# Encoder states loaded with channels first instead of transposed by TensorE

## The chip, the cores and the metric

The kernel runs on one core of a Trainium2 chip. The metric is device time in microseconds, the median of several executions. The core has five engines, each with its own queue of instructions: TensorE (PE, with its weight loads shown as PEld), VectorE (DVE), ScalarE (ACT), GpSimd (POOL) and SyncE (SP), which here only issues DMA transfers. Transfers run on 16 DMA engines.

## The reference, cut to what matters

The kernel is one decoder layer on x of shape (32, 128, 128), with a second input ctx_768 of shape (32, 128, 96), the encoder states. Everything is float32.

```
x = x + attn(layernorm(x))             # linear attention over 16 heads, gated
x = x + xattn(layernorm(x), ctx_768)   # the part that the change touches
x = x + ffn(layernorm(x))              # shared expert + one of 8 routed experts

def xattn(h, e, Wq, Wk, Wv, Wo, bo):   # h (32,128,128), e (32,128,96)
    q, k, v = h @ Wq, e @ Wk, e @ Wv   # 1024 wide: 16 heads of 64
    p = softmax(q @ k.T / 8) per head
    return (p @ v) @ Wo + bo
```

Keys and values are both products of the encoder states e with weights. On TensorE both operands of a product have the summed dimension on the partitions. For keys and values that is the channel of e (96), so the kernel needs e with channels first: `eT`, 96 partitions, and along the free dimension the positions of the group's four batch entries.

## The kernel before, in words

The 32 batch entries go in 8 groups of 4 (`NG`, `GT`); a group has 4 x 128 = 512 tokens (`GW`). Each group goes through self-attention (`attention`), the layer norm and query transposition for cross-attention (`prologue`), cross-attention proper, and the router (`router`); the expert part follows when all groups are routed.

Cross-attention is a loop over 64 steps, one for each group, half of the heads and batch entry, two steps per iteration (`for a in range(0, n, 2)`); a group so takes four iterations. An iteration computes scores, the maximum, exponentials, the division on POOL, the transposition of the probabilities, the mix with the values and the projection. Into fixed places of it (`place("S1")`, `place("P1")`, ...) go pieces of self-attention and prologue of the group two ahead and of the router of a group behind. `keys` for step a + 6 and `values` for the step itself are the products that read `eT`: so the first read of a group's `eT` is three iterations ahead of its own steps, and the last is `values` of its last step.

The order on PE, DVE, ACT and POOL is written out by hand: the wrapper `InTurn` (line 40, under which the profile shows all these instructions) ties each instruction of an engine behind the one before. SP's order is left to the framework's planner. In the trace SP issues what has nothing to wait for well ahead of its place in the code.

The encoder states before: `load_e(g)` (L229) loads a group of e as it lies, tokens on partitions, into `eg`, two buffers. Group 0's four blocks are transposed on TensorE by `encoder`; those of the other groups in step P2 of `attention(g)`, into the second bank of the PSUM pair that also holds the output projection (`oep`). In step E3 ACT copies them to `eT` (two buffers), and the load of the group two ahead is issued. On SP there are also the loads of x, the weights, and `clear_sorted`: 66 transfers of 264 KB that fill the DRAM table `xsort` (L324), into which POOL later scatters token rows (`indirect_dma_start` in `router`), each behind the clears ahead of it in the code.

Of the kernel before, what the change touches and what calls it, by code (L numbers as in the profile page):

```python
# [10 lines left out]
F32 = mybir.dt.float32  # L11
# [39 lines left out]
def kernel(  # L51
# [31 lines left out]
    nc = tc.nc  # L83
    B, S, D = x.shape
    DE = enc.shape[2]
# [7 lines left out]
    GT = 4  # L93
    NG = B // GT
    GW = GT * S
# [106 lines left out]
    pe = second_part.enter_context(tc.tile_pool(name="pe", bufs=2))  # L202
# [18 lines left out]
    bq_c = column(a_bq, "bq_c", nc.scalar)  # L221


    eg_of = {}

    def load_e(g):
        if g < NG:
            t = pe.tile([P, GT, DE], F32, tag="eg", name=f"eg{g}")
            nc.sync.dma_start(  # L229
                out=t, in_=enc[g * GT : (g + 1) * GT].rearrange("b s d -> s b d")  # L230
            )
            eg_of[g] = t
# [84 lines left out]
    def clear_sorted(g):  # L317

        n = GT * S
        first = [e * CAP + g * n for e in range(NE)]  # L320
        if g == NG - 1:
            first += range(NE * CAP, NROW, n)
        for r in first:
            ins = nc.sync.dma_start(  # L324
                out=xsort[r : r + n].rearrange("(p k) d -> p k d", p=P), in_=zeros
            )
            for put in sorted_by:
                tc.declare_no_dep(ins.ins, put.ins, reason="those rows lie in front")
            cleared_by.append(ins)
# [53 lines left out]
    def transposed(src, n, rows, name, ps=None, first=0):  # L383

        ps = bank(name) if ps is None else ps
        for t in range(first, first + n):
            pe_.transpose(ps[0:rows, t * P : (t + 1) * P], src[:, t, :], ident)
        return ps
# [15 lines left out]
    def attention(g, fixed=None):  # L404
# [73 lines left out]
        for a in range(2):  # L478
            nd2 = nd4[:, a, 0 : 2 * W].rearrange("p (b w) -> p b w", b=2)
            for b in range(2):  # L480
                t = 2 * a + b
# [47 lines left out]
        yield "E3"  # L529
        turned = None  # L530
        if g not in eT_of:
            eT_of[g] = pe.tile([DE, GW], F32, tag="eT", name=f"eT{g}")
            turned = act_.copy(eT_of[g], ep[0:DE, :])
            load_e(g + 2)
        ob = pa.tile([P, GT, D], F32, tag="ob", name=f"ob{g}")
        made = dve.tensor_tensor(
            ob, op4, bo_a.unsqueeze(1).to_broadcast([P, GT, D]), ALU.add
# [9 lines left out]


    steps = [(g, s, b) for g in range(NG) for s in range(2) for b in range(GT)]
    eT_of, xnT_of, qk_of, asked = {}, {}, {}, set()  # L550

    def encoder(g, evict):

        eT = pe.tile([DE, GW], F32, tag="eT", name=f"eT{g}")
        eT_of[g] = eT
        evict(eT, transposed(eg_of[g], GT, DE, f"eTp{g}")[0:DE, :])
        load_e(g + 2)

    def prologue(g, fixed=None):

# [31 lines left out]
    def queries(g, s, j):  # L592

        cols = slice((4 * s + j) * P, (4 * s + j + 1) * P)
        asked.add((g, s, j))
        qp = bank(f"xqp{g}_{s}_{j}")
        pe_.matmul(qp, lhsT=wq_x[:, cols], rhs=xnT_of[g], start=True, stop=True)
        act_.activation(qk_of[g, s, j][:, 0, :], qp, AF.Copy, scale=QSCALE)
# [17 lines left out]
    def scores(k):  # L616

        g, s, b = steps[k]
        rows = slice(b * S, (b + 1) * S)

        sc = pair(k % 2, f"sc{k}")
        for j in range(4):
            for p in range(2):
                half = slice(p * DH, (p + 1) * DH)
                pe_.matmul(
                    sc[:, p, j * P : (j + 1) * P],
                    lhsT=qk_of[g, s, j][half, 0, rows],
                    rhs=qk_of[g, s, j][half, 1, rows],
                    start=True,
                    stop=True,  # L630
                )
        sc_of[k] = sc

    def largest(k):
        sc = sc_of[k]
        nmax = small.tile([P, 8], F32, tag="nmax", name=f"nmax{k}")
        dve.tensor_reduce(
            nmax,
            sc.rearrange("p a (j k) -> p (a j) k", j=4),
            AX.X,  # L640
            ALU.max,
            negate=True,
        )
        pr_of[k] = pb.tile([P, 2, 4, P], F32, tag="pr", name=f"pr{k}")
        sums_of[k] = small.tile([P, 8], F32, tag="sums", name=f"sums{k}")
        sc_of[k] = sc, nmax
# [28 lines left out]
    def mix(k):  # L675

        av = bank(f"avp{k}")
        v, prT = v_of.pop(k), prT_of.pop(k)
        for j in range(4):
            for p in range(2):  # L680
                h = 2 * j + p
                pe_.matmul(
                    av[p * DH : (p + 1) * DH, j * P : (j + 1) * P],
                    lhsT=v[:, h * DH : (h + 1) * DH],
                    rhs=prT[:, p, j * P : (j + 1) * P],
                    start=True,
                    stop=True,
                )
        oT_of[k] = pb.tile([P, 4, S], F32, tag="oT", name=f"oT{k}")
        dve.tensor_copy(oT_of[k].rearrange("p j s -> p (j s)"), av)  # L690
# [436 lines left out]
    def place(*which):  # L1127
        for at in which:
            for one in list(beside):
                if one[0] == at:  # L1130
                    one[0] = next(one[1], None)
                    if one[0] is None:
                        beside.remove(one)
                        if one[2] is not None:
                            begin(one[2]())
# [69 lines left out]
    for a in range(0, n, 2):  # L1205
        both = (a, a + 1)
        scores(a)
        scores(a + 1)
        largest(a)
        place("S1")  # L1210
        if a:
            mix(a - 2)
            mix(a - 1)
        place("S3")
        largest(a + 1)
        exponentials(a)
        for k in both:
            if k + GT < n and steps[k + GT] not in asked:
                queries(*steps[k + GT])
        place("M1")  # L1220
        divide(a)
        if a:
            project(a - 2)
            project(a - 1)

            if a % 8 == 2 and 2 < a < n - 8 or a == n - 8:
                begin(router(steps[a - 1 if a == n - 8 else a - 3][0]))
        for k in both:
            if k not in v_of:
                values(k)  # L1230
        side["now"] = 0
        place("P1")
        if a >= n - 4:
            within["pair"] = 0
            products()
        exponentials(a + 1)
        divide(a + 1)
        place("E2")
        if a == n - 2:
            next(begun[0][1])  # L1240
        if a == 0:
            for k in (GT + 2, GT + 3):
                queries(*steps[k])
        for k in both:
            if k + GT + 2 < n and steps[k + GT + 2] not in qk_of:
                keys(*steps[k + GT + 2], act_.copy)
            if k == a:
                turn(a)
        if a == 0:
            values(2)  # L1250
        if a == n - 2:
            early = router(NG - 1, slice(0, GT // 2))
            next(early)
            next(early)
        place("S2", "M2")
        side["now"] = 1
        place("P2")
        if a >= n - 6:
            within["pair"] = 1
            products()  # L1260
        place("E3")
        if a == n - 2:
            next(begun[1][1])
            finish()
        while begun and a < n - 2:
            finish()
        turn(a + 1)
        if a == 0:
            place("S1")
        if a % 8 == 2:  # L1270
            clear_sorted(a // 8)
            g = a // 8 + 2
            if g < NG:
                begin(attention(g), lambda g=g: prologue(g))
        if a == 12:
            load_ffn()
        if a == n - 8:

            first_part.close()
            pools["g"] = ctx.enter_context(tc.tile_pool(name="pg", bufs=2, side="right"))  # L1280
            pools["c"] = ctx.enter_context(tc.tile_pool(name="pc", bufs=4, side="right"))
            pd = ctx.enter_context(tc.tile_pool(name="pd", bufs=1, side="right"))
            pools["down"] = pd.tile([P, NE, NC, D], F32, tag="wdr", name="wdr")
            for c in range(NC):
                nc.sync.dma_start(
                    out=pools["down"][:, :, c],
                    in_=rt_down[:, c * P : (c + 1) * P, :].rearrange("e p d -> p e d"),
                )
            whole_experts(pd, "up", rt_up)

            pieces += [
                (g, down(g) if c is None else hidden(g, c))
                for g, c in (
                    (0, 0), (0, 1), (1, 0), (1, 1), (2, 0), (2, 1), (0, None),
                    (3, 0), (3, 1), (1, None), (2, None), (3, None),
                )
            ]
# [198 lines left out]
```

## Time and profile before

| what | us |
|---|---|
| median of 3 runs | 613.0 (612.84 to 614.5) |
| the profiled execution | 612.94 |
| its span | 611.2 |
| PE busy | 594.8 |
| DVE busy | 443.0 |
| ACT busy | 390.9 |
| POOL busy | 247.9 |
| granted TensorE clock | 1.0 of full speed |

How to read it: busy is the time in which an engine has an instruction in work; weight loads (PEld) overlap products (PE). The span is that of the profiled instructions. In views of waits, `A <- B` reads "A stood idle until B was done". An `L40` in front of an engine's name is the wrapper's line, so instructions are told apart by the tiles that they write and read, `out<-in`. For DMA the page gives queues (q1 is SP's, q10 ACT's, q0 POOL's) with packets, megabytes, and the share of 16 engines' time that the packets took. In the first 75 us of the span the DMA engines are nearly full with the loads of x and weights and the clears; from then to about 410 us they are nearly idle, with 1 to 25 GB/s.

### The profile page before, as it was taken

How to read it: one execution, taken by the hardware profiler on the slowest of the kernel's cores; microseconds unless marked ns; L12 is line 12 of the kernel's file. 1: busy time of each engine (PE TensorE's matmuls, PEld its weight loads, DVE VectorE, ACT ScalarE, POOL GpSimd, SP SyncE). 2: the span in 40 equal slices, each digit the busy share in tenths (PEclk: the TensorE clock that was granted, in tenths of full speed). 3: DMA queues.
4: the chain of work that ended last, by engine and by line, in shares of the span. 5: the costliest groups of instructions: out<-in, count | busy, mean ns of one | idle time of the engine just before them, and what ended most of it. 6: DMA issues, size and time to landing. Idle time of an engine off the chain costs nothing. (4 is left out here: it accounts for less than half of the span.)

```text
span 611.2 us, 13300 instructions
## 1 busy us (share of the span) xinstructions
PE 594.8 (97%) x4681; PEld 449.6 (74%) x4681; DVE 443.0 (72%) x1226; ACT 390.9 (64%) x1414; POOL 247.9 (41%) x248
## 2 busy tenths in 40 slices
PE   8999999999999999999999999999999999899997
PEld 7546777776777777776777777767777777699965
DVE  5757667868877787778786878697776687866645
ACT  3376776777677767776777677766766676256521
POOL 3133423433544344424452445244434344346651
PEclk9999999999999999999999999999999999999999
DMA  6999900000000000000000000005000002054137
GB/s 161 304 354 352 354 25 2 14 2 1 10 23 1 1 11 23 1 2 10 23 2 1 10 10 1 1 11 146 2 2 10 10 10 79 28 119 118 49 101 210
DMA packets 42659, 39.64 MB, mean 65 GB/s; under 512 B 8592, under 2 KB 32656, under 8 KB 42592
## 3 DMA queue, kind: packets, MB, share of 16 engines
q1 hardware_dynamic: 39168, 33.80, 18.3%
q0 software_dynamic: 2144, 4.46, 2.2%
q8 instruction: 38, 0.62, 0.4%
q10 hardware_dynamic: 1280, 0.53, 0.4%
q14 instruction: 29, 0.24, 0.1%
HBM read 14.37 MB, written 24.40 MB: 63 GB/s over the span
## 5 line engine op out<-in xcount | busy, mean ns | idle before, releaser
L40 ACT ACTIVATE pr<-sc,nmax 128x128 f32<-128x128 f32 x512 | 180.5, 387 | 46.6 <-DVE nmax L40 43.7
L40 POOL TENSOR_TENSOR pr<-pr,rs 128x1024 f32<-128x1024 f32 x64 | 121.2, 1897 | 140.0 <-DVE x L40 87.8
L40 ACT ACTIVATION_READ_ACCUMULATOR pr<-sc,nmax 128x1 f32 x512 | 115.7, 226 | 0.0
L40 DVE TENSOR_REDUCE nmax<-sc 128x8 f32<-128x1024 f32 x64 | 77.9, 1218 | 12.7 <-PE sc L40 12.6
L40 PEld LDWEIGHTS xyp<-wo_x,oT 128*128 128x128 f32 x512 | 61.9, 192 | 14.1 <-issue 13.4
L40 PE MATMUL sc<-qk 64*128 64x128 f32 x1024 | 66.0, 279 | 0.7 <-DVE act L40 0.7
L40 PE MATMUL xkp<-eT,wk_x 96*128 96x512 f32 x128 | 65.1, 593 | 0.0
L40 PEld LDWEIGHTS sc<-qk 64*128 64x128 f32 x1024 | 59.9, 187 | 6.7 <-issue 5.0
L40 PE MATMUL xqp<-xnT_b,wq_x 128*128 128x512 f32 x128 | 63.1, 617 | 0.7 <-ACT xnT_b L40 0.7
L40 PE MATMUL avp<-prT,v 128*64 128x128 f32 x1024 | 63.2, 276 | 0.0
L40 PE MATMUL xyp<-wo_x,oT 128*128 128x128 f32 x512 | 62.7, 276 | 0.1
L40 PE MATMUL vp<-wv_x,eT 96*128 96x512 f32 x128 | 60.5, 593 | 0.8 <-ACT qk L40 0.8
L40 PEld LDWEIGHTS avp<-prT,v 128*64 128x64 f32 x1024 | 55.2, 137 | 4.1 <-issue 0.2
L40 ACT COPY prT<-prTb 128x512 f32<-128x512 f32 x64 | 37.6, 588 | 31.3 <-PE prTb L40 31.3
L40 DVE COPY prT<-prTa 128x512 f32<-128x512 f32 x64 | 43.8, 686 | 17.1 <-PE prTa L40 16.7
L40 ACT COPY qk<-xkp 128x512 f32<-128x512 f32 x64 | 37.7, 589 | 28.9 <-PE xkp L40 28.4
L40 DVE COPY v<-vp 128x512 f32<-128x512 f32 x64 | 43.4, 689 | 16.1 <-PE vp L40 16.1
L40 PEld LDWEIGHTS prTa<-ident,pr 128*128 128x128 f32 x256 | 30.6, 141 | 30.1 <-issue 16.7
L40 DVE COPY oT<-avp 128x512 f32<-128x512 f32 x64 | 42.2, 685 | 4.8 <-PE avp L40 4.6
L40 POOL DMA_INDIRECT ytok<-yt,rows x35 | 33.6, 961 | 25.8 <-DVE rows L40 23.7
L40 POOL DMA_INDIRECT xsort<-xs,row x32 | 32.4, 1012 | 20.9 <-issue 8.8
L40 PE MATMUL prTa<-ident,pr 128*128 128x128 f32 x256 | 39.1, 275 | 1.4 <-POOL pr L40 1.3
(170 smaller groups left out, 1010.0 us busy)
## 6 DMA issues: line engine op xcount, KB each, us to landing
xsort<-zeros SPq DMA_DIRECT2D x66, 264.0 KB, 4.0
xt<-xsort SPq DMA_DIRECT2D x39, 66.0 KB, 2.2
yg<-ytok SPq DMA_DIRECT2D x8, 256.0 KB, 4.8
x<-in_x_dram SPq DMA_DIRECT2D x7, 256.0 KB, 5.3
out_dram<-x SPq DMA_DIRECT2D x7, 256.0 KB, 4.9
eg<-in_ctx_dram SPq DMA_DIRECT2D x8, 192.0 KB, 3.3
wdr<-in_L_ffn_rt_down_dram SPq DMA_DIRECT2D x2, 512.0 KB
up<-in_L_ffn_rt_up_dram SPq DMA_DIRECT2D x1, 1024.0 KB, 9.2
```

Of the source, the lines that this page charges most:

```text
L40: made = getattr(self.engine, name)(*operands, **more)
```

## The change

Groups 2 to 7 no longer load `eg`. For them `load_e` issues four transfers, one for each batch entry, that write `eT` itself: 96 partitions of 128 words each, where neighbouring words of a partition lie 384 bytes apart in DRAM. `eT` has three buffers instead of two. `load_e` is called once per group in the loop, at the end of its second iteration (a % 8 == 2), just ahead of the clears, instead of behind a transposition. In `attention`, the transposes and the ACT copy drop out wherever `eT_of` has the group, which is the case for groups 2 to 7; group 0 and group 1 are loaded and transposed as before.

```
     def load_e(g):
-        if g < NG:
+        if 2 <= g < NG:
+            t = pe.tile([DE, GT, S], F32, tag="eT", name=f"eT{g}", bufs=3)
+            for b in range(GT):
+                nc.sync.dma_start(
+                    out=t[:, b, :], in_=enc[g * GT + b].rearrange("s d -> d s")
+                )
+            eT_of[g] = t.rearrange("p b s -> p (b s)")
+        elif g < 2:
             t = pe.tile([P, GT, DE], F32, tag="eg", name=f"eg{g}")
...
         if g not in eT_of:
-            eT_of[g] = pe.tile([DE, GW], F32, tag="eT", name=f"eT{g}")
+            eT = pe.tile([DE, GT, S], F32, tag="eT", name=f"eT{g}", bufs=3)
+            eT_of[g] = eT.rearrange("p b s -> p (b s)")
             turned = act_.copy(eT_of[g], ep[0:DE, :])
-            load_e(g + 2)
...
     def encoder(g, evict):
-        eT = pe.tile([DE, GW], F32, tag="eT", name=f"eT{g}")
-        eT_of[g] = eT
+        eT = pe.tile([DE, GT, S], F32, tag="eT", name=f"eT{g}", bufs=3)
+        eT_of[g] = eT = eT.rearrange("p b s -> p (b s)")
         evict(eT, transposed(eg_of[g], GT, DE, f"eTp{g}")[0:DE, :])
-        load_e(g + 2)
...
         if a % 8 == 2:
+            load_e(a // 8 + 2)
             clear_sorted(a // 8)
```

More of the change, by code (lines that the diff above doesn't have):

```diff
@@ L221 @@
     bq_c = column(a_bq, "bq_c", nc.scalar)
-    eg_of = {}
+    eg_of, eT_of = {}, {}
     def load_e(g):
-        if g < NG:
+        if 2 <= g < NG:
[6 more added lines that the diff above has]
+        elif g < 2:
             t = pe.tile([P, GT, DE], F32, tag="eg", name=f"eg{g}")
@@ L549 @@
     steps = [(g, s, b) for g in range(NG) for s in range(2) for b in range(GT)]
-    eT_of, xnT_of, qk_of, asked = {}, {}, {}, set()
+    xnT_of, qk_of, asked = {}, {}, set()
     def encoder(g, evict):
-        eT = pe.tile([DE, GW], F32, tag="eT", name=f"eT{g}")
-        eT_of[g] = eT
+        eT = pe.tile([DE, GT, S], F32, tag="eT", name=f"eT{g}", bufs=3)
+        eT_of[g] = eT = eT.rearrange("p b s -> p (b s)")
         evict(eT, transposed(eg_of[g], GT, DE, f"eTp{g}")[0:DE, :])
-        load_e(g + 2)
     def prologue(g, fixed=None):
```

## The prediction

> **What bounds the kernel now.** I read the page's busy shares, then TensorE's (PE's) timeline around one transposition, the encoder tile, SP's timeline, and the DMA answers for two short stretches. From the page:
>
> ```profile
> PE 594.8 (97%) x4681; PEld 449.6 (74%) x4681; DVE 443.0 (72%) x1226; ACT 390.9 (64%) x1414; POOL 247.9 (41%) x248
> ```
>
> PE is busy nearly always, the others are not. Its timeline (start, length, what; no bracket at the end means no idle time before it), from 85 us on:
>
> ```profile
> 85.63 1.88 PE L40 MATMUL vp<-wv_x,eT 96*128 96x512 f32 x4
> ...
> 106.00 1.05 PE L40 MATMUL oep<-wo_a,gT 128*128 128x128 f32 x8
> 106.89 0.60 PE L40 MATMUL oep<-ident,eg 128*96 128x128 f32 x4
> 107.33 0.60 PE L40 MATMUL prTa<-ident,pr 128*128 128x128 f32 x4
> ...
> 117.94 1.02 PE L40 MATMUL xkp<-eT,wk_x 96*128 96x512 f32 x2
> ...
> 179.88 1.02 PE L40 MATMUL xkp<-eT,wk_x 96*128 96x512 f32 x2
> ...
> 427.63 1.02 PE L40 MATMUL xkp<-eT,wk_x 96*128 96x512 f32 x2
> ```
>
> Three things are to be seen. The four transposes of a group take PE from 106.89 to 107.33, 0.44 us, since they are pipelined. A group lasts 61.94 us (117.94 to 179.88). And 117.94, 179.88 and so on to 427.63 are the first key products of groups 2 to 7: the moments at which their eT must be there. The line at 85.63 holds the last products that read eT of group 0; they end near 87.5.
>
> The encoder tile, and SP's timeline:
>
> ```profile
> L40 PE MATMUL oep<-ident,eg x28: 272/273/273, 47.7 to 416.9; 128*96 128x128 f32 x28
> L229 SPq DMA_DIRECT2D eg<-in_ctx_dram x8: 368/390/711, 1.3 to 293.3; - x8
> ...
> DMA to landing us min/median/max: 2.6/3.3/8.6
> ```
> ```profile
> 22.75 0.37 SPq L229 DMA_DIRECT2D eg<-in_ctx_dram  x1
> 23.21 11.97 SPq L324 DMA_DIRECT2D xsort<-zeros  x16
> ...
> 54.76 20.59 SPq L324 DMA_DIRECT2D xsort<-zeros  x27
> 107.52 186.19 SPq L229 DMA_DIRECT2D eg<-in_ctx_dram  x4
> 418.81 0.99 SPq L1285 DMA_DIRECT2D wdr<-in_L_ffn_rt_down_dram  x2
> ```
>
> An encoder load lands in 3.3 us now and nobody feels it. SP issues everything that waits for nothing at once: the 66 clears of xsort are issued between 23 and 75 us, 52 us of moving, though the code has them spread over the groups. From 107 to 418 us SP has only four loads to issue.
>
> The DMA answer for 107.5 to 111.5 us, in which one encoder load moves alone, and for 9.6 to 9.8 us, where the one-column biases arrive, 4 bytes a packet:
>
> ```profile
> q1 hardware_dynamic: 528, 0.20, 20.8%
> ```
> ```profile
> DMA packets 54, 0.00 MB, mean 1 GB/s; under 512 B 54, under 2 KB 54, under 8 KB 54
> q1 hardware_dynamic: 54, 0.00, 12.6%
> ```
>
> The share is of 16 engines' time. A 384-byte row takes an engine 0.208 x 4 us x 16 / 528 = 25 ns. A 4-byte word takes it 0.126 x 0.2 us x 16 / 54 = 7.5 ns. But the words come only 54 in 0.2 us, 3.7 ns apart over all engines: one in 59 ns per engine, with the engine idle between.
>
> **The change part by part.**
>
> Removed on PE: 4 transposes in each of 6 groups (28 in the oep row are groups 1 to 7; group 1 keeps its own, as does group 0 outside the row). 6 x 0.44 = 2.6 us. From 62 to 120 us PE is busy 58.00 of 58.00 us, so what goes from its row goes from the time. Bounds: 0 if another engine steps in, 6 x 0.60 = 3.6 us if the four cost their whole span. I take 2.6, the distance between starts.
>
> Removed on ACT: six copies of eT at 0.584 us, 3.5 us. ACT is at 64% and PE does not wait for these copies; nothing. Off DVE: the sum ob waited for the transposes of the same PSUM pair (11.2 us over seven); it starts about 0.44 us sooner, as PE's next work does; nothing.
>
> Added and moved on SP: 24 loads for 6, 0.39 us each to issue, 9 us on a queue idle for 300 us; nothing, unless issuing so many words holds SP longer, which is then hidden behind the transfer itself. What stands behind them on SP are clears, the shared expert's weights, and from 418 us on the expert weights. No load waits for a TensorE transposition now, but from group 3 on each waits for the last reader of the buffer three groups back: 87.5 us for group 3, needed at 179.9, so 92 us of room, at one load per 61.9 us.
>
> The unknown is the transfer. Each load has 96 x 128 = 12,288 words; a group has 49,152, and 3,072 per engine. Call a group's time L. By the words' own 7.5 ns, L = 23 us. By the 25 ns of a strided row, L = 77 us. By the 59 ns at which the column's words came, L = 181 us. What L may be: the group 2 load starts near 23 us and has to be in by 117.9, so L up to 95. If all clears follow it on the same queue (52 us), later loads end at 75 + 2L (needed 179.9, L up to 52), 75 + 3L, ... 75 + 6L (needed 427.6, L up to 59). So from 52 to 59 us a group, 17 to 19 ns a word, loads turn from hidden to bound. I take 7.5 ns: it is the only row that has words, and in the burst a pace below that of an idle engine says that eight words per engine came too thinly, not that the engine could take no more. The other two ends stay for the range.
>
> New wait: the first key product of a group waits for four landings instead of one ACT copy. PE goes in the written order, so scores, mixes and projections queue behind it, and ACT, DVE and POOL behind those. If on time it costs at most one 0.2 us gap (the longest "issue" gap of PE's weight loads) in six groups, 1.2 us; I take nothing, as PE has no idle time in that stretch although those gaps occur.
>
> Sum: the profiled execution took 612.94 us (span 611.2, 1.7 around it), the median of the runs is 613.0. 612.94 - 2.6 = 610.3 us. The hidden case's own range is 609.0 (a gain of 3.6 and the 0.2 by which two runs differ) to 612.0 (the gaps paid in part).
>
> **The rivals.**
>
> DMA bound at the pace of strided rows: 25 ns a word, L = 77. The last group's states are in at 75 + 6 x 77 = 537 instead of 427.6, less the gain: 610.3 + 109 = 719 us. For it: every strided read in the trace has that price or more, and the words of a row are read by all engines at the same place. Against it: 7.5 ns of occupancy, with 25 in bytes and not in overhead. It decides from L = 59. The Trainium skill (VectorE: DVE Perf Modes, section The three transpose paths) says that a plain copy whose strides do the transposing is 19 times slower than the hardware transpose, which it puts at 1309 ns for 128x128 two-byte elements. As an estimate that is 24.9 us for 16,384 elements, 18.7 for a load here, 75 a group, and 706 us in this sum; no transfer in this trace transposes, so nothing here shows it.
>
> Much worse: 59 ns a word, L = 181. 75 + 1086 - 428 = 733 us late, 1343 us in all. For it: that is how words arrive. Against it: only 128 in a load, eight per engine, start and end included.
>
> Clears late: POOL scatters the first sorted rows at 153.2 us and must find the clears landed. If SP takes the third group's load (at 87.5) ahead of the clears that those rows need, with L = 23 the 52 us of clears end at 162, 9 us late; POOL's divisions stand behind its scatters, PE behind them: 619 us. Against it: clears wait for nothing and were issued far ahead.
>
> PE not the bound: the transposes go and nothing moves, 613.0. For it: weight loads are busy only 74%. The Trainium skill (Perfetto Trace Analysis, section Identifying the Most-Contended Engine) says that matmul busy share misleads and that weight loads measure better. Against it: PE's view of waits has 3.1 us of idle time in all between 60 and 420 us.
>
> **How the numbers follow.** Hidden 0.47, strided pace 0.25, column pace 0.18, clears late 0.06, PE not the bound 0.04. About 0.3%, 1.8 us, is what a measurement can tell from no change. Within hidden, a gain of 2.6 stands 0.8 above that, so 0.36 goes to faster and 0.11 to same; same is 0.15 with the last case; the rest is slower, 0.49. So the likeliest single mechanism is a gain, while the several ways to lose weigh more together. The range takes all but the column pace (0.18): 609 to 720 us.
>
> **What would show it.** Right: oep<-ident,eg with x4 instead of x28, some 295,000 more packets of 4 bytes on q1 at about 7.5 ns, DMA share in the slices up to a third between 100 and 420 us, groups 61.5 us apart, no wait of xkp for eT. Wrong: DMA share at 9 throughout, PE with idle time at the first xkp of a group ended by DMA eT, groups longer than 62 us; or POOL's scatters released by xsort<-zeros. What would make the prediction wrong above all is words that take an engine over 19 ns.

## The result and the profile after

The changed kernel takes 610.22 us (median; 610.01 to 611.67) against 612.92 for the kernel before measured with it: a ratio of 0.9958, 95% interval 0.9947 to 0.9968, 2.7 us less. In a second series it came to 610.48 against 613.17 (0.9957, interval 0.994 to 0.9974).

The page of the kernel after, busy times, DMA slices and queues:

```profile
PE 593.2 (97%) x4657; PEld 446.7 (73%) x4657; DVE 442.6 (73%) x1226; ACT 386.8 (63%) x1408; POOL 247.5 (41%) x248
...
DMA  5999999991990199009900990005000002144137
...
q1 hardware_dynamic: 331296, 33.80, 57.5%
...
eT<-in_ctx_dram SPq DMA_DIRECT2D x24, 48.0 KB, 16.5
```

PE has 24 instructions fewer and is as full as before. SP's queue q1 moves the same 33.80 MB in 292,000 more packets. The DMA slices, 15.2 us each, now stay full up to 137 us, where the words of groups 2 and 3 run among the clears, and then show four pulses with gaps between them, one each for groups 4 to 7, where there were nearly none. PE's timeline of the kernel after, around the place where the transposes stood, and the first key products of groups 2, 3 and 7:

```profile
107.61 1.05 PE L40 MATMUL oep<-wo_a,gT 128*128 128x128 f32 x8
108.50 0.60 PE L40 MATMUL prTa<-ident,pr 128*128 128x128 f32 x4
...
119.11 1.02 PE L40 MATMUL xkp<-eT,wk_x 96*128 96x512 f32 x2
...
180.58 1.02 PE L40 MATMUL xkp<-eT,wk_x 96*128 96x512 f32 x2
...
426.48 1.02 PE L40 MATMUL xkp<-eT,wk_x 96*128 96x512 f32 x2
```

prTa follows oep directly. None of these key products has a bracket, and in the view of the tile xkp no key product at all waits for a load. A group lasts 61.47 us, 0.47 less than the 61.94 before.

The first of these lines lie later than before (119.11 against 117.94), although less work precedes them: in this execution, which took 611.67 us, PE's eight query products at 31.73 us took 5.39 us instead of 3.70, under a granted clock of 0.86 in the stretch of 28 to 40 us. On most chips here the executions of one kernel, the one before included, fall into two heaps about 1.7 us apart, so single times are not compared below. In the profile of the repeat, without that dip, the same product of group 2 stands at 117.41 us, and 424.83 us in place of 426.48.

SP's timeline of the kernel after:

```profile
23.38 12.05 SPq L332 DMA_DIRECT2D xsort<-zeros  x16
...
37.12 19.05 SPq L332 DMA_DIRECT2D xsort<-zeros  x25
56.22 22.68 SPq L231 DMA_DIRECT2D eT<-in_ctx_dram  x4
78.94 26.58 SPq L332 DMA_DIRECT2D xsort<-zeros  x25
105.62 249.34 SPq L231 DMA_DIRECT2D eT<-in_ctx_dram  x20
```
```profile
L231 SPq DMA_DIRECT2D eT<-in_ctx_dram x24: 312/6500/8388, 56.2 to 348.6; - x24
```

The planner put group 2's load behind 41 of the clears, not ahead of them. The second view gives the time that SP spends on one of these loads, in ns (least, median, most): 6.5 us at the median, where a load of `eg` took 0.39 us. The clears behind group 2's load were so issued up to 104.8 us instead of 74.6. And the DMA answer for 211 to 240 us, one group's words:

```profile
DMA  0899999999998999999618999999999999999998
DMA packets 49183, 0.52 MB, mean 18 GB/s; under 512 B 49115, under 2 KB 49115, under 8 KB 49179
...
q1 hardware_dynamic: 49051, 0.20, 140.7%
```

Each slice is 0.725 us; all but the first, one near 226 us and a bit of the last are nearly full. So a group's 49,152 words pass in about 28.2 us: 9.2 ns for a word on each of 16 engines, 7.0 us for a load. This is a mean over the pulse: of its stretches of 2 us, 213 to 215 us has 4,973 words (6.4 ns) and 217 to 219 us has 2,445 (13 ns). The share of 140.7% says that the packets' recorded times overlap: 1.407 x 29 us x 16 / 49,051 = 13.3 ns is how long a word is in work, not how far apart words are.

### The profile page after: what moved, and what is told of

Same layout as the page of the kernel before. It is cut to its first block, busy times and chain, and to the rows that moved or that the text cites. A ratio compares the mean times of both kernels' runs of the same rounds, so it can differ in the third digit from the quotient of the medians.

```text
span 609.9 us, 13273 instructions
## 1 busy us (share of the span) xinstructions
PE 593.2 (97%) x4657; PEld 446.7 (73%) x4657; DVE 442.6 (73%) x1226; ACT 386.8 (63%) x1408; POOL 247.5 (41%) x248
## 3 DMA queue, kind: packets, MB, share of 16 engines
q1 hardware_dynamic: 331296, 33.80, 57.5%
## 5 line engine op out<-in xcount | busy, mean ns | idle before, releaser
L40 PEld LDWEIGHTS xyp<-wo_x,oT 128*128 128x128 f32 x512 | 61.9, 192 | 14.1 <-issue 13.4
L40 PE MATMUL xqp<-xnT_b,wq_x 128*128 128x512 f32 x128 | 64.8, 631 | 0.7 <-ACT xnT_b L40 0.7
```

Of the source, the lines that this page charges most:

```text
L40: made = getattr(self.engine, name)(*operands, **more)
```

## Experiments

The theory: the gain is PE's 6 x 0.44 us and nothing else, and the words cost nothing because a group's 28 us of them lie inside its 62 us. Rivals: part of the gain comes from ACT's copy or from the changed order; the words do cost something, covered by a larger gain; the room is smaller or larger than the arithmetic of needed and free says.

### Which part of the removed work was the gain

Given back, transposes and copy:

```diff
         if g not in eT_of:
             ep = transposed(eg_of[g], GT, DE, "", oe[:, 1])
+        else:
+            ep = transposed(eg_of[g % 2], GT, DE, "", oe[:, 1])
...
             turned = act_.copy(eT_of[g], ep[0:DE, :])
+        else:
+            turned = act_.copy(
+                eg_of[g % 2].rearrange("p t d -> p (t d)")[0:DE], ep[0:DE, 0 : GT * DE]
+            )
```

> The changed kernel with the removed work given back: in groups 2 to 7 the four transposes (of an older eg tile) into the same PSUM bank, and an ACT copy out of it, 384 columns wide, into that eg tile, which nobody reads; eT still comes word by word. Theory (the words cost nothing, the gain is TensorE's 6 x 0.44 us): back at the time of the kernel before, 612.9 us (612.4 to 613.4). Rival (the words cost something that the gain covers): above 613.5. Rival (the gain comes from elsewhere, as the planner's order or the loads): stays at 610.2.

Measured: ratio to the kernel before 1.0014 (1.0002 to 1.0026), 613.8 us in terms of 612.9.

Only the transposes, without the two lines of the copy:

> The changed kernel with only the transposes given back in groups 2 to 7 (into the same PSUM bank, read by nobody), no ACT copy. Theory (TensorE's share is the whole gain): 612.9 us (612.4 to 613.4). Rival (half or more of the gain comes from the ACT copy and the sum that waited beside it): 611.5 or less.

Measured: 613.29 us, ratio 1.0004 (0.9991 to 1.0016). PE's timeline of this kernel has the 0.44 us back, and the groups are 61.9 us apart again (118.36 to 427.94 for five):

```profile
106.42 1.06 PE L40 MATMUL oep<-wo_a,gT 128*128 128x128 f32 x8
107.31 0.60 PE L40 MATMUL oep<-ident,eg 128*96 128x128 f32 x4
107.75 0.60 PE L40 MATMUL prTa<-ident,pr 128*128 128x128 f32 x4
...
118.36 1.02 PE L40 MATMUL xkp<-eT,wk_x 96*128 96x512 f32 x2
...
427.94 1.02 PE L40 MATMUL xkp<-eT,wk_x 96*128 96x512 f32 x2
```

Both edits reach one group more than meant. Group 0 has its `eT` from `encoder` before its self-attention comes to this place, so it too takes the new branch, and gets four transposes that it has neither in the kernel before nor in the changed one. The row has 32 products, where the kernel before has 28:

```profile
L40 PE MATMUL oep<-ident,eg x32: 272/273/273, 24.9 to 417.2; 128*96 128x128 f32 x32
```

The extra four stand at 24.94 us, and by group 1's first key product this kernel is 0.43 us later than the one before (57.77 against 57.34).

Only an ACT copy:

```diff
             turned = act_.copy(eT_of[g], ep[0:DE, :])
+        else:
+            act_.copy(
+                eg_of[g % 2].rearrange("p t d -> p (t d)")[0:DE], gT[0:DE, 0 : GT * DE]
+            )
```

> The changed kernel with only an ACT copy given back in groups 2 to 7, at the same place, 384 columns wide, from gT to an old eg tile that nobody reads. Theory: 610.2 us, within 0.5. Rival (ACT's copy is half or more of the gain): 611.5 or more.

Measured: 610.3 us, ratio 0.9957 (0.9941 to 0.9974), as the changed kernel. Here too there are seven copies, one of them in group 0.

So with the words in place, giving back PE's transposes gives back the whole gain, and giving back a copy on ACT gives back none of it. With seven groups given back and six removed, 0.44 us above the kernel before is to be expected, a ratio of 1.0007, and both intervals hold it; groups 2 to 7 are 61.92 us apart in the kernel with both, as before. So the 613.8 us, above the 613.5 at which the expectation saw a cost of words, is no sign of one. The sum ob on DVE waits for the given-back transposes too (12.2 us over eight), so no run parts it from them; but PE, in the changed kernel (3.9 us) as before (3.1), has little idle time between 60 and 420 us, and none of it at these places.

### Whether the words cost anything

```diff
-            for b in range(GT):
-                nc.sync.dma_start(
-                    out=t[:, b, :], in_=enc[g * GT + b].rearrange("s d -> d s")
-                )
+            flat = enc[g * GT : (g + 1) * GT].rearrange("b s d -> (b s d)")
+            nc.sync.dma_start(
+                out=t.rearrange("p b s -> p (b s)"),
+                in_=flat.rearrange("(p f) -> p f", p=DE),
+            )
```

> The changed kernel with one load of long rows per group (512 words on each of 96 partitions, in the order of DRAM) in place of the four loads of words; what lands in eT is then not the transposed states, so the transposition is left out altogether. Theory (the words are hidden whole): 610.2 us, within 0.5. Rival (the words cost x by contention on queues, memory or waits): 610.2 - x, with x over 0.5.

Measured: 619.84 us, ratio 1.0099 (1.0079 to 1.0118), against every expectation. The reason is a confound of the experiment: with other states in eT other experts are picked, and one product group of the expert part shows it (the lines of the kernel before and of this one, from the views of that tile):

```profile
L40 PE MATMUL rgu<-xT,wt x280: 275/275/281, 535.2 to 584.3; 128*128 128x128 f32 x140
```
```profile
L40 PE MATMUL rgu<-xT,wt x312: 275/275/377, 534.5 to 593.8; 128*128 128x128 f32 x156
```

The conditional four last tiles are in work, and their part ends 9.5 us later. The time of the whole therefore says nothing on words. The stretch ahead of it does tell: the first key products of groups 2 and 7 in the kernel with rows,

```profile
119.22 1.02 PE L40 MATMUL xkp<-eT,wk_x 96*128 96x512 f32 x2
...
426.70 1.02 PE L40 MATMUL xkp<-eT,wk_x 96*128 96x512 f32 x2
```

are 307.48 us apart, and with words 307.37. With long rows instead of 292,000 single words, five groups take the same time to 0.1 us. The words are hidden whole in this stretch, and SP issues the last of their loads at 348.6 us, inside it.

### How much room there is

Two buffers instead of three (`bufs=2` at the three places of eT):

> The changed kernel with two buffers of eT instead of three. A load then waits for the last reader two groups back instead of three: group 3's from about 149 us on, needed at 180.6, so 31 us of room. Theory (a group's words pass in 28 us, plus 2 us to land): on the edge, 610 to 614 us, gaps of at most 1 us at the first key product of a group. Rival (the packets' own mean of 13 ns counts, 41 us a group): 10 us late in each group, 660 us or more.

This kernel, those with doubled and tripled loads and the first one with group 1 by words ran on a chip on which the kernel before takes 623.16 us (in the profile of this run the products rgu of the expert part spread over 57 us instead of 49), so ratios count. Measured: 1.0011 (0.9987 to 1.0034); in terms of 612.9 us that is 613.6. About the whole gain is lost, and not much more. PE's timeline shows where:

```profile
119.59 1.10 PE L40 MATMUL xkp<-eT,wk_x 96*128 96x512 f32 x2 [1.89 <-DMA eT<-in_ctx_dram]
...
181.52 1.10 PE L40 MATMUL xkp<-eT,wk_x 96*128 96x512 f32 x2 [0.33 <-DVE v L40]
...
429.13 1.10 PE L40 MATMUL xkp<-eT,wk_x 96*128 96x512 f32 x2
```

Group 2's load now has to wait until 87.57 us for group 0's buffer and comes 1.89 us late, more than the 1 us expected at most; from there on groups are 61.91 us apart, where three buffers give 61.48 on the same chip (the kernel with group 1 by words). The first key products of groups 3 to 6 each stand behind 0.2 to 0.5 us of idle time; the profile puts that down to DVE three times and to the load once, so that it is the load each time is not shown. A load of 28 us in 31 us of room is on the edge; one of 41 us, the rival's, would be 10 us late every time, and none is. This bears out the pace and shows what the third buffer is for.

Each load twice, and three times (`for b in 2 * list(range(GT))`, `3 * ...`):

> The changed kernel with every load of words issued twice (the second pass writes the same values), 56 us a group at 9.1 ns a word and engine. Theory: under the 62 us of a group, so nearly hidden: 610 to 620 us, with a wait at most in groups 2 and 3, whose loads share the queue with the clears. Rival (13 ns a word, 82 us a group): loads bound, 740 us or more.

> The changed kernel with every load of words issued three times, 84 us a group. Theory: over the 62 us of a group, loads bound; from 56 us on six times 84 and 19 us of clears, so group 7 is there at about 580 instead of 427 us: 740 to 780 us, with TensorE idle at the first key product of groups 3 to 7 for 20 us and more. Rival (words overlap in the queues, so that more of them cost less each): under 700 us.

Measured: twice, 1.0267 (1.0218 to 1.0315), 629 us in terms of 612.9; three times, 1.2893 (1.2832 to 1.2955), 790. PE's timelines, twice first:

```profile
197.72 2.04 PE L40 MATMUL xkp<-eT,wk_x 96*128 96x512 f32 x2 [16.95 <-DMA eT<-in_ctx_dram]
```
```profile
254.69 2.05 PE L40 MATMUL xkp<-eT,wk_x 96*128 96x512 f32 x2 [42.40 <-DMA eT<-in_ctx_dram]
```

Twice the words (57 us a group at 9.2 ns a word) wait once for 17 us, at group 3, whose load SP issues only from 135 us on, behind the last 24 clears, and 1.5 us at group 2; from group 4 on the groups are 61.5 us apart as if nothing were doubled. That is the shape expected, but the time is 9 us above the 620 that I gave as the most. Three times the words wait at every group, 170.9 us in six waits, and groups 3 to 7 lie 88.3 us apart on the mean. It is more than the 84 expected, and the total is above my 780: over 170 to 430 us a word took 9.6 ns on the mean, and the slices of this kernel, 1 us each from 300 to 340 us, show short gaps that are counted in:

```profile
DMA  9992299999959999991199999929999995999999
```

Between 57 and 88 us a group the load turns into the bound; that it does so at the group's 62 us fits, but no run shows the place.

### What sets a word's pace

```diff
-                    out=t[:, b, :], in_=enc[g * GT + b].rearrange("s d -> d s")
+                    out=t[:, b, :],
+                    in_=bass.AP(
+                        tensor=enc.tensor,
+                        offset=first * DE,
+                        ap=[[7 * DE + 1, DE], [DE, S]],
+                    ),
```

> The changed kernel with the same number of words from other places: partition d starts 7 d rows further on, so that the engines do not read one row of DRAM at the same time. What lands in eT is then not the transposed states. Theory (a word's pace is the engine's cost of one): 28 us a group as before, 9.1 ns a word and engine. Rival (reads of the same place get in each other's way): under 24 us a group.

Measured, from one profiled execution: the window of 210 to 239 us of this kernel,

```profile
DMA  7899999997979999998159899999999999999991
...
q1 hardware_dynamic: 49159, 0.20, 132.9%
```

28 us, 9.2 ns a word, as when the 96 partitions read the words of the same rows.

```diff
-                    out=t[:, b, :], in_=enc[g * GT + b].rearrange("s d -> d s")
+                    out=t[:, b, :].rearrange("p (s two) -> p s two", two=2),
+                    in_=bass.AP(
+                        tensor=enc.tensor,
+                        offset=(g * GT + b) * S * DE,
+                        ap=[[1, DE], [2 * DE, S // 2], [1, 2]],
+                    ),
```

> The changed kernel with eT filled from half as many pairs of neighbouring words (8 bytes each), so with wrong values, the transposition is left out. Theory (cost per piece, not per byte): 14 us a group. Rival (cost per word): 28 us a group.

Measured, from one profiled execution: the window of 210 to 225 us,

```profile
DMA  0399999990769999991799459999639989999411
...
q1 hardware_dynamic: 24625, 0.20, 98.0%
```

Half the pieces in about 13.7 us, 8.9 ns a piece, at twice the bytes each. In these two places and at these two sizes, the price is of the piece. Why a piece costs this much, and why the pace changes within a pulse, these runs don't show.

### One group more

```diff
-        if 2 <= g < NG:
+        if 1 <= g < NG:
...
-        elif g < 2:
+        elif g < 1:
```

> The changed kernel with group 1 loaded word by word too (condition 1 <= g). TensorE loses four more transposes, 0.44 us. The load stands behind wq_x, wv_x and wo_x and ahead of x of groups 2 to 7, and is needed at the first key product of group 1, near 57 us. Theory: its 28 us of words are in at about 45 us; 609.8 us. Rival (words among full queues take twice as long, 56 us from 15 us on): a wait of up to 15 us there, 615 to 625 us.

Measured: 0.9949 (0.9923 to 0.9975). Then beside the changed kernel on one chip:

> The changed kernel again, beside the next one on the same chip. Theory: 0.9958 of the kernel before (0.995 to 0.997).

> Group 1 by words too, beside the changed kernel on the same chip. Theory: one more group of 0.44 us, 0.0007 below the changed kernel's ratio, which five rounds can hardly tell from none. Rival (the first 57 us, where the queues are full, give it back): equal to or above the changed kernel's ratio, with a gap at TensorE's first key product of group 1 or at group 2's first normalization.

Measured: changed kernel 610.48, 0.9957 (0.994 to 0.9974); with group 1 by words 610.09, 0.9951 (0.9934 to 0.9968). The difference has the expected size, 0.4 us, and can't be told from none by the times. In the profiles group 2's first key product is at 117.10 instead of 117.41, and group 7's at 424.61 instead of 424.83, so there are 0.2 to 0.3 us, and no wait for a load in the first 57 us.

## Why the prediction was right, point by point

**The gain, 2.6 us: right.** 610.3 was forecast, 610.22 measured. PE's distance between starts, not the 0.60 us of the four, was the size to take: 0.47 us less per group. That the total agrees to 0.1 us is luck: the runs themselves spread from 610.01 to 611.67. The giving back of each part shows that the gain comes and goes with PE's transposes, and that ACT's copy was rightly put at nothing; for DVE's sum this follows from PE's timeline, not from a run of its own.

**PE as the bound: right.** The rival that weighed the 74% of the weight loads came to nothing: what went from a full PE went from the time. The Trainium skill (Perfetto Trace Analysis, Identifying the Most-Contended Engine) warns of matmul busy time as a measure of how near the ceiling a kernel is. That is another question than which engine the others wait for, and on that the view of waits, with 3.1 us of PE idle in 360, was the better witness here.

**The words' time, L = 23 us: right in kind, too small in size.** It is 28.2 us, because words pass 9.2 ns apart on the mean, while the 7.5 ns came from how long a few lone packets were in work. In the stream a packet is in work for 13.3 ns, and packets overlap; neither number is the pace. So the step took an occupancy for a pace, and the forecast held because there were 52 us of room for either. The choice between the three ends was right: at 9.2 ns in a full queue, the 59 ns were thin supply, as argued. That the 25 ns were bytes fits pairs and words at one price for a piece, but nothing between 8 and 384 bytes was run. The Trainium skill (VectorE: DVE Perf Modes, The three transpose paths) states its factor of 19 for a large innermost stride at the destination; here the destination is contiguous and the stride is in the source. The estimate worked out from it, 18.7 us for a load, is 2.7 times what the load's words took on the queue here, 7.0 us, so the measurement decides.

**Where loads begin to bind, 52 to 59 us a group: about right.** At 57 us one group in six was late by 17 us and one by 1.5, at 88 us all of them were late. But the order on SP was not the one I reckoned with: group 2's load began at 56 us, behind 41 clears, not at 23, and it took SP 6.5 us to issue one of its four, not the 0.39 of the sum. The sum had left that open as hidden behind the transfer, and so it was. It did no harm: its words were in at about 87 us, and the first product that needs them comes at 119.

**New wait, clears, scatters: right, nothing.** No xkp waits for a load; the first scatter is at 154.3 us in the profile above and at 152.7 in the repeat, against 153.2 before, and nobody waits for a clear. The bound of 1.2 us was read too low: the longest issue gap of the weight loads is 0.3 us in that view, not 0.2, which makes it 1.8; nothing of it came.

**What would show it.** The packets (292,000 more against 295,000) and the group length (61.47 against 61.5) came as said. The pace did not (9.2 ns, not 7.5), nor the DMA share: I wrote up to a third in the slices, and in a pulse nearly every slice is full, 28 of 62 us.

**Chances.** More weight stood on slower (0.49) than on faster (0.36). What separated them was one price, a word's pace, that the trace of before bounded only between 7.5 and 59 ns; the range reached to 720 for it. That width was the price of not knowing, and the row that proved nearest was the one with words in it, though its number was not a pace.

## What to carry to other kernels

Where one engine had no idle time in a stretch, work taken off it was worth its distance between starts, not its duration; a copy taken off another was worth nothing, and both could be tested by giving the parts back one at a time. When a part is given back, count its instructions in the profile: here it came back seven times instead of six. A load that is wasteful in bandwidth (0.2 MB in 28 us) cost nothing while it fitted the period of the loop and its buffers let it start early enough; count the pieces of such a load, not its bytes, and give it the buffer that makes the room. And an experiment that puts wrong data into a kernel with data-dependent work has to be read up to where the data decide.

## What the runs showed of the hardware

A load of single words, 384 bytes apart in DRAM, passes at 9.2 ns a word on each of 16 engines on the mean of a group (6.4 to 13 ns in stretches of 2 us), at 9.2 ns too with the partitions 7 rows apart, and at 8.9 ns a piece with pieces of 8 bytes. While one group's words run the DMA queue's share reads 133% to 141%, since recorded packet times overlap, so this share does not say how full the engines are. And after long idle times of PE, in the kernel with each load three times, the granted clock was low, and the two key products behind the wait took 2.05 us instead of 1.02; the windows of that kernel (start and end, length, busy time of PE, PEld, DVE, ACT and POOL, granted clock, DMA share, GB/s),

```profile
212.00:255.00 43.00, 0.60 (x4) 0.39 (x3) 0.69 (x2) 0.63 (x2) 3.36 (x3) 0.53 1.50 7
255.00:343.00 88.00, 63.07 (x497) 46.72 (x497) 47.99 (x128) 42.77 (x160) 25.68 (x20) 0.85 1.43 11
```

have 0.53 in a stretch with 0.6 us of PE work and 0.85 over the next group, of whose 88 us PE is busy 63.
